# The end of layer 3 in a four-layer graph network: one buffer for two copies, transposes moved and placed in another bank, two steps exchanged, scalar operations reordered

## The chip, the cores and the metric

The kernel runs on one core of one Trainium2 chip. The metric is device microseconds of one execution; lower is better. Beside the runs there is one execution taken by the hardware profiler, and every duration below comes from it.

## What is computed

A graph of 3327 nodes with 64 features per node passes through four layers over one dense 3327 x 3327 matrix `adj`. Each layer normalises the features, applies a rectifier, computes an update and adds it to `x`. Layer 3, where the change lies, works in hyperbolic space:

```python
x_tan = _logmap0(x, C)
left = x_tan @ att_W[:D] + att_b
right = x_tan @ att_W[D:]
adj_att = jax.nn.sigmoid(left + right.T) * adj
x_local = _logmap(x[:, None, :], x[None, :, :], C)
support_t = jnp.einsum('ij,ijd->id', adj_att, x_local)
return _proj(_expmap(x, support_t, C), C)
```

`_logmap(x_i, x_j)` is a combination of the two feature vectors `x_i` and `x_j`, so the weighted sum over j falls apart into a vector part (a matrix of weights times features) and scalar sums per node. `_expmap` and `_proj` then need, per node, a few dot products, one tanh, one square root and some twenty scalar operations. The output is `x` plus a multiple of the vector sum plus a multiple of the normalised features.

## The kernel before

The nodes are padded to 26 blocks of 128. They are split in two groups: `gs_`, 12 blocks, and `gf`, 14 blocks. Layers 0 to 2 stream `adj` through SBUF. Layer 3 works in 13 phases (0 to 12) on pairs of blocks, each in two halves (`b` or `k`, 0 and 1). A phase is made of steps: `distances` (TensorE), `gelus` and `square` (ScalarE), `tanh_d` and `tanh_t` (ScalarE), `attention_*` and `factors_*` (VectorE), `gather_*` (TensorE, the vector sums) and `singles` (TensorE, the scalar sums). A step with `d` serves the pairs as they are stored; a step with `t` serves the same pairs turned, with TensorE transposes in `turned`.

The order of all these steps is written out by hand in the string `ORDER3`. `singles.12.0`, for instance, is step `singles` of phase 12, half 0. Each engine executes its own instructions in that order, and waits for others by semaphores. The last lines of `ORDER3` are the ones that matter here. After them comes `finish()`, which no other work overlaps.

The vector sums of layer 3 are kept in PSUM: `x0` (bank 2) and `x1` (bank 3) for `gf`, `x2_` (bank 1) and the upper half of `ps_` (bank 0) for `gs_`. The lower half of `ps_` holds the scalar sums of all phases but the last half. The scalar sums of that last half go into `late_`, the first 256 columns of `ends_`, a pair of banks (`pair(0)`, 1024 columns). In its second bank lies `ds_` (columns 512 to 543), the scalar sums brought to one value per node.

The steps near the end, with their lines in the profile:

- `gather_d(12, 1)` first calls `copied_singles(0, ps_)`: ScalarE copies the lower half of `ps_` into the SBUF buffer `pp_` (L1625). Its gather matmuls (shown under the helper's line, L1493) then add into the upper half of `ps_`. All `singles` matmuls are also recorded under L1493, with `p2c` as an operand.
- `singles(12, 1, 0)` takes `ends_`, clears `late_` (L1298) and adds the turned pairs' sums; `singles(12, 1, 1)` first calls `picked(0)` (L1630, matmuls of the first copied sums into `ds_`), then adds the direct pairs' sums.
- The generators `e` (`finish_s`) and `f` (`finish_f`) copy finished vector sums to SBUF (`m_t`, L1664), multiply and square them (L1595, L1666, L1667) and add the products over the features with matmuls into `drows` (L1607, in bank 2).
- `finish()` does the same for the last columns (L1678 to L1680), copies the late single sums (L1625), adds the last products (L1607), copies `drows` into the SBUF buffer `dd` (L1684), and calls `picked(1)` (L1630). `dd` and `pp_` are separate leases of one buffer, tagged `sq`. Four matmul records bring the dot products to one value per node (L1688, into `dots`, in bank 2). The vector sums are turned to node order with 13 transposes, in three calls of `by_nodes` (L1619): 4 into bank 3, 3 into the second bank of `ends_`, 6 into pair 1.
- The scalar block follows on VectorE, on operands of 128 x 26: L1706 to L1720 up to a reciprocal, the tanh on ScalarE (L1721), L1724 to L1738, the square root on ScalarE (L1739), L1740 to L1743. Its results are the scalars `ch` and `ka`.
- The output: TensorE puts `xn` into two PSUM sums (L1751), ScalarE scales the features with `ch`, block by block (L1753), TensorE adds them (L1755), VectorE multiplies the vector sums with `ka` (L1758) and adds (L1761, L1769), and SyncE stores (L1764). `sums_x` names the two PSUM sums: bank 0 for blocks 12 to 19, bank 1 for blocks 20 to 25.

The calls in `finish()` that the change moves, as they stand before:

```python
        picked(1)
        v = dots.rearrange("p (j r i h) -> p i j r h", j=2, i=2, h=2)
...
        by_nodes(gf, late_f[0], bank(3), 0, 4)
        by_nodes(gf, late_f[0], ends_[:, 5 * P :], 4, gf.n)
        by_nodes(g, m, pair(1), 0, g.n)
        sums_x = [(12, 20, bank(0)), (20, NB, bank(1)[:, : 6 * D])]
...
        V.tensor_mul(b_, ds, qs)
        V.tensor_mul(e_, ds, xq)
        V.tensor_mul(su, ss, Bq2)
```

Of the kernel before, what the change touches and what calls it, by code (L numbers as in the profile page):

```python
# [12 lines left out]
AF = mybir.ActivationFunctionType  # L13
OP = mybir.AluOpType
# [4 lines left out]
D = 64  # L19
P = 128  # L20
NB = 26
# [19 lines left out]
FAC = MIN_NORM  # L41
ATH = 8.31776613691702
MAX_NORM = 1.0 - 0.004
# [31 lines left out]
GROUPS = [Group(0, 6), Group(6, HB)]  # L75
# [149 lines left out]
def order3(text):  # L225
# [127 lines left out]
    turned.12.1.0 f tanh_d.12.0 attention_d.12.0 f singles.11.1 singles.11.0 tanh_t.12.1.0  # L353
    tanh_t.12.1.1 attention_t.12.1 e factors_t.12.1.0 turned.12.1.1 gather_t.12.1.0
    factors_d.12.0 gather_d.12.0 e factors_t.12.1.1 tanh_d.12.1 attention_d.12.1
    gather_t.12.1.1 singles.12.1.0 factors_d.12.1 singles.12.0 gather_d.12.1 gather_t.12.0.1
    singles.12.1.1 e e e e n s b f f f f f e
    """
)
# [72 lines left out]
def gnn_kernel(ctx: ExitStack, tc: tile.TileContext, t, out):  # L432
    nc = tc.nc
    V, S, G, T = nc.vector, nc.scalar, nc.gpsimd, nc.tensor
# [97 lines left out]
    ident = p0.tile([P, P], F32, name="ident")  # L532
# [75 lines left out]
    def big(g, name):  # L608

        if g.part is None:  # L610
            a = p0.tile([P, GROUPS[1].nb, D], F32, name=name, tag="b_" + name)
        else:

            if name not in bigs:
                bigs[name] = p0.tile([P, GROUPS[1].nb, D], F32, name=name, tag="b_" + name)
            a = bigs[name][:, 6 * g.part :, :]
        return a[:, : g.nb, :]

    def flat(a):
        return a.rearrange("p a d -> p (a d)")  # L620

    def pair(i):

        return ps.tile([P, 1024], F32, name="pair", tag=f"pair{i}")

    def bank(i):
        return ps.tile([P, 512], F32, name="bank", tag=f"bank{i}")
# [174 lines left out]
    gs_, gf = GROUPS  # L802
# [46 lines left out]
    for i, (ca, cb) in enumerate(starts):  # L849
        g = Group(ca, cb, part=i % 2)  # L850
# [643 lines left out]

    @step3
    def gather_d(m, b):
        nonlocal pp_
        if (m, b) == (n_all - 1, 1):
            assert ("singles", m, 0) in made3
            pp_ = flat(big(GROUPS[1], "sq"))[:, : 4 * P].rearrange("p (s i c) -> p s i c", s=2, i=2)  # L1500
            copied_singles(0, ps_)
        a = columns(dirs[m, b], PHASES[m].n)
        for c, ts, first in PHASES[m].runs:
            for p, o, lo, hi in runs(ts, place):
                for k in range(2):
                    add(
                        p[k * D : (k + 1) * D, o : o + (hi - lo) * P],
                        xd[:, 2 * c + b, :],
                        a[:, k, (first + lo) * P : (first + hi) * P],
                    )  # L1510
# [105 lines left out]
    def by_nodes(g, m, out_, lo, hi):  # L1616

        for c in range(lo, hi):
            T.transpose(  # L1619
                out_[:, (c - lo) * P : (c - lo + 1) * P], m[:, c * P : (c + 1) * P], ident  # L1620
            )
        nat.append((2 * (g.c0 + lo), 2 * (g.c0 + hi), out_[:, : (hi - lo) * P]))
# [16 lines left out]
    nat, drows, dots = [], None, None  # L1639
# [32 lines left out]
    late_ends, late_f = None, [None]  # L1672

    def finish():
        g = gs_
        m, w1, w2 = late_ends
        cs = slice(4 * P, 6 * P)
        S.activation(m[:, cs], ps_[:, 2 * P :], AF.Copy)  # L1678
        V.tensor_mul(w1[:, cs], xs[:, cs], m[:, cs])
        S.activation(w2[:, cs], m[:, cs], AF.Square)  # L1680
        copied_singles(1, late_)
        added(g, (w1, w2), 2)
        dd = flat(big(GROUPS[1], "sq"))[:, 4 * P : 6 * P]
        S.activation(dd, drows, AF.Copy)  # L1684
        picked(1)
        v = dots.rearrange("p (j r i h) -> p i j r h", j=2, i=2, h=2)
        for i in range(2):
            T.matmul(  # L1688
                v[:, i],
                lhsT=dd[:, i * P : (i + 1) * P],  # L1690
                rhs=ident.rearrange("p (j h k r) -> p j k r h", j=2, h=2, k=4)[:, :, 0],
                start=True,
                stop=True,
            )
        by_nodes(gf, late_f[0], bank(3), 0, 4)
        by_nodes(gf, late_f[0], ends_[:, 5 * P :], 4, gf.n)
        by_nodes(g, m, pair(1), 0, g.n)
        sums_x = [(12, 20, bank(0)), (20, NB, bank(1)[:, : 6 * D])]
        ds, hs, ss = ds_[:, :NB], dots[:, :NB], dots[:, 32 : 32 + NB]


        f = wide3("f", "d2")
        b_, e_, hu, su, p1, d_, Bp, th, y2, xy, ka, den, ch, n2 = (
            f[:, i * NB : (i + 1) * NB] for i in range(14)
        )
        V.tensor_mul(b_, ds, qs)  # L1706
        V.tensor_mul(e_, ds, xq)
        V.tensor_mul(su, ss, Bq2)
        V.scalar_tensor_tensor(b_, hs, 0.25 * HK, b_, op0=OP.mult, op1=OP.subtract)
        V.scalar_tensor_tensor(e_, hs, 0.25 * HK, e_, op0=OP.mult, op1=OP.subtract)  # L1710
        V.scalar_tensor_tensor(hu, hs, 0.125 * HK, B1, op0=OP.mult, op1=OP.mult)
        V.tensor_mul(d_, b_, e_)
        V.tensor_scalar(p1, su, -(FAC**2), 1.0, op0=OP.mult, op1=OP.add)
        V.tensor_sub(hu, e_, hu)

        V.scalar_tensor_tensor(Bp, d_, -(FAC**2), p1, op0=OP.mult, op1=OP.add)
        V.tensor_add(su, su, d_)
        V.scalar_tensor_tensor(th, Bp, MIN_NORM, rpn, op0=OP.max, op1=OP.mult)
        V.scalar_tensor_tensor(hu, hu, 2.0 * FAC, rpn, op0=OP.mult, op1=OP.mult)
        V.reciprocal(th, th)  # L1720
        S.activation(th, th, AF.Tanh)  # L1721


        V.tensor_mul(y2, th, th)  # L1724
        V.tensor_mul(xy, th, hu)
        V.tensor_mul(th, th, rpn)
        V.scalar_tensor_tensor(den, su, FAC**2, y2, op0=OP.mult, op1=OP.mult)
        V.scalar_tensor_tensor(n2, y2, 1.0, Bp, op0=OP.subtract, op1=OP.mult)
        V.scalar_tensor_tensor(ka, xy, 1.0, y2, op0=OP.add, op1=OP.add)
        V.scalar_tensor_tensor(den, den, 1.0, xy, op0=OP.add, op1=OP.add)  # L1730
        V.scalar_tensor_tensor(ch, ka, FAC * MAX_NORM, b_, op0=OP.mult, op1=OP.mult)
        V.scalar_tensor_tensor(n2, den, MIN_NORM, n2, op0=OP.max, op1=OP.add)
        V.tensor_scalar(den, den, MIN_NORM, None, op0=OP.max)
        V.scalar_tensor_tensor(th, Bp, MAX_NORM, th, op0=OP.mult, op1=OP.mult)
        V.tensor_mul(n2, n2, den)
        V.scalar_tensor_tensor(den, den, MAX_NORM**2, den, op0=OP.mult, op1=OP.mult)
        V.tensor_mul(ka, ka, alq)
        V.tensor_max(n2, n2, den)  # L1738
        S.activation(n2, n2, AF.Sqrt)  # L1739
        V.tensor_add(ch, ch, th)  # L1740
        V.reciprocal(n2, n2)
        V.tensor_mul(ch, ch, n2)
        V.tensor_mul(ka, ka, n2)  # L1743
        w1, w2 = (
            wide3("w", sb(n_all, b))[:, : NB * D].rearrange("p (k d) -> p k d", d=D)
            for b in range(2)
        )


        for lo, hi, a in sums_x:  # L1750
            T.matmul(a, lhsT=ident, rhs=flat(xn[:, lo:hi]), start=True, stop=False)  # L1751
        for k in [*range(12, NB), *range(6)]:
            S.activation(w2[:, k, :], h[:, k, :], AF.Copy, scale=ch[:, k : k + 1])  # L1753
        for lo, hi, a in sums_x:
            T.matmul(a, lhsT=ident, rhs=flat(w2[:, lo:hi]), start=False, stop=True)  # L1755

        def times(lo, hi, a):
            V.tensor_mul(w1[:, lo:hi], a.rearrange("p (k d) -> p k d", d=D), bc(ka[:, lo:hi]))  # L1758

        def plus(lo, hi, a):  # L1760
            V.tensor_add(w1[:, lo:hi], w1[:, lo:hi], a)  # L1761

        def store(lo, hi):
            nc.sync.dma_start(out[:, lo:hi, :], w1[:, lo:hi])  # L1764

        (_, _, a), *larger = nat[::-1]
        times(6, 12, a[:, 6 * D :])
        plus(6, 12, xn[:, 6:12])
        V.tensor_mul(w2[:, 6:12], h[:, 6:12], bc(ch[:, 6:12]))  # L1769
        plus(6, 12, w2[:, 6:12])  # L1770
        store(6, 12)
        for lo, hi, b in larger[::-1]:
            times(lo, hi, b)
        times(0, 6, a[:, : 6 * D])
        plus(0, 6, xn[:, 0:6])
        for lo, hi, b in sums_x:
            plus(lo, hi, b.rearrange("p (k d) -> p k d", d=D))
            store(lo, hi)
        plus(0, 6, w2[:, 0:6])
        store(0, 6)  # L1780
# [28 lines left out]
        nonlocal within_  # L1809
        within_ = nc.values_load(within, min_val=0, max_val=1)  # L1810

    x0 = x1 = ps_ = x2_ = late_ = ds_ = pp_ = ends_ = None
    cf = ctx.enter_context(ExitStack())
    c2 = ctx.enter_context(ExitStack())
    if True:
# [104 lines left out]
        if True:  # L1920
# [6 lines left out]
            h = n3.tile([P, NB, D], F32, name="h3")  # L1927
# [10 lines left out]
            x2, qs, pn, rpn, lefts, righth, B1, Bq2, alq, xq = (  # L1938
                n3.tile([P, NB], F32, name=n)
                for n in "x2 qs pn rpn left righth B1 Bq2 alq xq".split()  # L1940
            )
# [429 lines left out]
```

## Time and profile before

| | |
|---|---|
| median of 3 runs | 647.39 us (647.32 to 648.18) |
| the profiled execution | 643.85 us |
| its span, first to last instruction | 642.0 us |
| TensorE busy in the span | 601.1 us (94%) |
| VectorE busy | 450.2 us (70%) |
| ScalarE busy | 378.4 us (59%) |
| mean granted TensorE clock | 0.989 |
| first instruction of the scalar block (L1706) | at 625.28 us |
| first scaled block of the output (L1753) | at 630.07 us |
| end of the last VectorE instruction | at 636.55 us |

Times within the trace are microseconds from the span's start. A matrix product of 32-bit numbers shows as two records in the trace. The busy share of an engine is a mean over stages with different limits: in the last 28 us, where the change lies, the engines take turns, and what counts is what each of them waits for. The profile names those waits by the engine and line that ended them.

### The profile page before, as it was taken

Reading aid. Unit: us, or ns where it says so; the run is one execution under the profiler, and the core shown is the slowest. Engines: PE = TensorE matmul, PEld = TensorE weight load, DVE = VectorE, ACT = ScalarE, POOL = GpSimd, SP = SyncE. Lnnn points to the kernel's source line nnn. Section 1 sums busy time; section 2 is a strip of 40 time slices with the busy share of each in tenths; the row PEclk is TensorE's granted clock in tenths of the full one; section 3 lists DMA queues with packets and bytes.
Section 4 is the critical chain, followed back from the end, with each engine's and each line's share of the span. In section 5 each row is a group of like instructions: output and inputs, shape, how many; then the busy total and the mean of one; then the engine's idle time right before and its main releaser. Section 6 shows DMA issues by size and latency. Waiting matters only on the chain.

```text
span 642.0 us, 13208 instructions
## 1 busy us (share of the span) xinstructions
PE 601.1 (94%) x5592; PEld 321.8 (50%) x5592; DVE 450.2 (70%) x687; ACT 378.4 (59%) x528; POOL 25.3 (4%) x48
## 2 busy tenths in 40 slices
PE   2987999899998999999999999989999999999992
PEld 1442444334332433346777776546655555556660
DVE  3230876454488760567864866999999999999955
ACT  3110400130254420369987979999999998999734
POOL 0000000000000000030000010017000000000000
PEclk9999999999999999999999999989999999999996
DMA  8999999449998799999978895519676776755401
GB/s 334 415 417 418 364 393 339 177 157 392 418 417 368 282 415 419 417 365 400 359 277 292 300 329 225 189 58 288 206 246 211 251 235 226 240 177 196 153 2 59
DMA packets 32531, 183.40 MB, mean 286 GB/s; under 512 B 3696, under 2 KB 4752, under 8 KB 32464
## 3 DMA queue, kind: packets, MB, share of 16 engines
q1 hardware_dynamic: 32112, 181.63, 75.4%
q0 software_dynamic: 352, 0.85, 0.5%
q8 instruction: 45, 0.74, 0.5%
q14 instruction: 22, 0.18, 0.1%
HBM read 180.76 MB, written 0.85 MB: 283 GB/s over the span
## 4 chain that ended last, share of the span: by engine, by line
PE 78%; DMA 8%; DVE 6%; ACT 5%; issue 1%; SPq 0%; DVEq 0%; ACTq 0%
PE bank L772 25%; PE bank L1493 18%; PE pair L1368 8%; DMA adj<-in_adj 8%; PE bank L1886 7%; PE pair L1864 7%; PE pair L1483 4%; PE pair L873 3%; ACT w L1876 2%; PE pair L677 1%; DMA xn<-in_x 1%; PE bank L647 1%; PE bank L1755 1%; ACT tr L1438 0%; DVE mask L1833 0%
## 5 line engine op out<-in xcount | busy, mean ns | idle before, releaser
L772 PE MATMUL bank<-adj,m_a 128*64 128x384 f32 (+1 forms) x832 | 153.5, 516 | 8.9 <-DMA adj<-in_adj 6.5
L772 PEld LDWEIGHTS bank<-adj,m_a 128*64 128x64 f32 x832 | 57.1, 137 | 95.0 <-issue 71.3
L1876 ACT ACTIVATE w<-pair,ebias 128x896 uint16<-128x896 f32 (+1 forms) x100 | 90.1, 953 | 14.6 <-PE pair L1864 14.4
L772 PE MATMUL bank<-adj,m_b 128*64 128x384 f32 (+1 forms) x416 | 76.7, 515 | 1.4 <-ACT hm L861 1.4
L499 DVE SCALAR_TENSOR_TENSOR edges<-adj,edges 128x1792 bf16<-128x1792 f32 (+1 forms) x24 | 45.0, 1890 | 31.3 <-DMA adj<-in_adj 31.2
L1833 DVE TENSOR_SCALAR mask<-adj 128x1792 bf16<-128x1792 f32 (+1 forms) x52 | 51.7, 1025 | 18.4 <-PE pair L1864 18.2
L861 ACT ACTIVATE hm<-bank 64x384 f32<-64x384 f32 (+1 forms) x8 | 4.1, 512 | 94.5 <-DVE mh L860 94.2
L1886 PE MATMUL bank<-w,m_b 128*64 128x384 bf16 (+1 forms) x416 | 55.9, 340 | 0.1
L772 PEld LDWEIGHTS bank<-adj,m_b 128*64 128x64 f32 x416 | 28.8, 137 | 45.8 <-issue 41.5
L1368 PE MATMUL pair<-xs 64*128 64x384 f32 (+3 forms) x120 | 50.8, 507 | 0.5 <-ACT s L1384 0.5
L1368 PE MATMUL pair<-xs,xw 64*128 64x384 f32 (+3 forms) x120 | 50.8, 507 | 0.0
L1409 ACT ACTIVATE d<-leftb,righth 128x768 f32<-128x768 f32 (+3 forms) x45 | 38.7, 918 | 0.1
L1886 PE MATMUL bank<-w,h_t 128*64 128x384 bf16 (+1 forms) x208 | 38.2, 339 | 0.1
L1449 DVE SCALAR_TENSOR_TENSOR d<-d,adj 128x1792 f32<-128x1792 f32 x19 | 38.3, 2014 | 0.0
L1864 PE MATMUL pair<-mask,tri_b 128*64 128x384 bf16 (+1 forms) x208 | 37.0, 339 | 0.0
L1864 PE MATMUL pair<-mask,rest_a 128*64 128x384 bf16 x192 | 33.5, 341 | 0.1
L1493 PE MATMUL bank<-d,xd 128*64 128x384 f32 (+3 forms) x236 | 32.2, 411 | 0.5 <-ACT sq L1625 0.5
L1886 PEld LDWEIGHTS <-m_b 128*64 128x64 bf16 x416 | 27.3, 110 | 10.6 <-issue 1.5
L1490 DVE SCALAR_TENSOR_TENSOR tr<-pair,tr 128x1024 f32<-128x1024 f32 (+3 forms) x28 | 26.7, 954 | 4.0 <-PE pair L1483 3.5
L1438 ACT ACTIVATE tr<-leftb,righth 128x512 f32<-128x512 f32 (+1 forms) x48 | 28.7, 660 | 0.4 <-PE bank L1493 0.4
L1493 PE MATMUL bank<-d,p2c 128*32 128x128 f32 (+1 forms) x348 | 28.5, 322 | 0.0
L1864 PE MATMUL pair<-mask,tri_a 128*64 128x384 bf16 x208 | 25.8, 341 | 0.7 <-ACT w L1876 0.7
(371 smaller groups left out, 1089.0 us busy)
## 6 DMA issues: line engine op xcount, KB each, us to landing
adj<-in_adj SPq DMA_DIRECT2D x108, 896.0 KB, 6.5
adj<-in_adj SPq DMA_DIRECT2D x94, 768.0 KB, 8.7
adj<-in_adj SPq DMA_DIRECT2D x8, 640.0 KB, 5.1
adj<-in_adj SPq DMA_DIRECT2D x2, 512.0 KB, 3.9
xn<-in_x SPq DMA_DIRECT2D x3, 192.0 KB, 4.8
out<-s SPq DMA_DIRECT2D x3, 192.0 KB, 2.6
xw<-xs POOLq DMA_DIRECT2D x4, 128.0 KB, 4.9
w_l<-in_w_l SPq DMA_DIRECT2D x1, 460.0 KB, 9.9
```

What stands on the lines that cost most here:

```text
L499: V.scalar_tensor_tensor(e, a, 0.0, e, op0=OP.not_equal, op1=OP.add)
L772: T.matmul(acc[q][h * D : (h + 1) * D, : hi - lo], lhsT=m[:, k, :], rhs=a[:, h * g.w + lo : h * g.w + hi], start=first, stop=last,)
L1368: T.matmul(p[k][:, o : o + n], lhsT=l, rhs=r, start=not rows, stop=rows)
L1409: S.activation(columns(dirs[m, b], ph.n)[:, :, first * P : first * P + n], left_of(ph.g)[:, :, o : o + n], AF.Tanh, bias=righth[:, 2 * c + ...
L1438: S.activation(by_rows(a, m, u)[:, x : x + 2 * n].rearrange("p (b e) r c -> p b e r c", b=2), left_of(ph.s)[:, :, o : o + n * P].rearrange ...
L1449: V.scalar_tensor_tensor(a[:, :w], a[:, :w], 1.0, stream.tile(stream.now), op0=OP.add, op1=OP.mult)
L1490: V.scalar_tensor_tensor(a, p, rest_of(m), a, op0=OP.add, op1=OP.mult)
L1493: T.matmul(out, lhsT=lhsT, rhs=rhs, start=False, stop=True, skip_group_check=True)
L1833: V.tensor_scalar(masks[n][:, :w], a, 0.0, None, op0=OP.not_equal)
L1864: T.matmul(cnt[h][s * D : (s + 1) * D, P + lo : P + hi], lhsT=l, rhs=r, start=first and j == 0, stop=j == len(terms) - 1 or first and s == ...
L1876: S.activation(w, e, AF.Relu, bias=ebias)
L1886: T.matmul(acc2[i][q][h * D : (h + 1) * D, : hi - lo], lhsT=p[:, 2 * c + a, :], rhs=ws[n][:, h * g.w + lo : h * g.w + hi].bitcast(BF16), s ...
```

## The change

Four edits, all of them between the last steps of phase 12 and the square root of the scalar block:

1. In `ORDER3`, `singles.12.0` moves ahead of `singles.12.1.0` and `factors_d.12.1`. Before, it stood behind both.
2. The buffer for the copied single sums is taken once, in `gather_d(12, 1)`, and the copy of `drows` goes into its columns 512 to 767 under the name `dd_`. Before, `finish()` took a new lease of the same buffer for it.
3. In `finish()`, `b_` and `e_` are issued ahead of the dot product matmuls, and the 13 transposes behind the first VectorE operations that read the dot products. The three transposes of blocks 20 to 25 go to bank 0 in place of the second bank of `ends_`, and the output sum of blocks 12 to 19 goes to the first bank of pair 0 in place of bank 0.
4. The scalar operations are reordered; none is added, none is left out. `p1` goes ahead of `d_`, and `su` and `hu` behind the tanh; after the tanh, the operations that lead to the square root go first, and `ch`, `th` and `ka` go behind it. The multiplication of `th` by `rpn` moves down.

```diff
-    gather_t.12.1.1 singles.12.1.0 factors_d.12.1 singles.12.0 gather_d.12.1 gather_t.12.0.1
+    gather_t.12.1.1 singles.12.0 singles.12.1.0 factors_d.12.1 gather_d.12.1 gather_t.12.0.1
...
-            pp_ = flat(big(GROUPS[1], "sq"))[:, : 4 * P].rearrange("p (s i c) -> p s i c", s=2, i=2)
+            ends = flat(big(GROUPS[1], "sq"))
+            pp_ = ends[:, : 4 * P].rearrange("p (s i c) -> p s i c", s=2, i=2)
+            dd_ = ends[:, 4 * P : 6 * P]
             copied_singles(0, ps_)
...
-        dd = flat(big(GROUPS[1], "sq"))[:, 4 * P : 6 * P]
-        S.activation(dd, drows, AF.Copy)
+        S.activation(dd_, drows, AF.Copy)
         picked(1)
-        v = dots.rearrange("p (j r i h) -> p i j r h", j=2, i=2, h=2)
-        for i in range(2):
-            T.matmul(
-                v[:, i],
-                lhsT=dd[:, i * P : (i + 1) * P],
...
-        by_nodes(gf, late_f[0], bank(3), 0, 4)
-        by_nodes(gf, late_f[0], ends_[:, 5 * P :], 4, gf.n)
-        by_nodes(g, m, pair(1), 0, g.n)
-        sums_x = [(12, 20, bank(0)), (20, NB, bank(1)[:, : 6 * D])]
         ds, hs, ss = ds_[:, :NB], dots[:, :NB], dots[:, 32 : 32 + NB]
...
         V.tensor_mul(b_, ds, qs)
         V.tensor_mul(e_, ds, xq)
+        v = dots.rearrange("p (j r i h) -> p i j r h", j=2, i=2, h=2)
+        for i in range(2):
+            T.matmul(
+                v[:, i],
+                lhsT=dd_[:, i * P : (i + 1) * P],
...
         V.tensor_mul(su, ss, Bq2)
         V.scalar_tensor_tensor(b_, hs, 0.25 * HK, b_, op0=OP.mult, op1=OP.subtract)
         V.scalar_tensor_tensor(e_, hs, 0.25 * HK, e_, op0=OP.mult, op1=OP.subtract)
         V.scalar_tensor_tensor(hu, hs, 0.125 * HK, B1, op0=OP.mult, op1=OP.mult)
+        by_nodes(gf, late_f[0], bank(3), 0, 4)
+        by_nodes(gf, late_f[0], bank(0), 4, gf.n)
+        by_nodes(g, m, pair(1), 0, g.n)
+        sums_x = [(12, 20, pair(0)[:, :512]), (20, NB, bank(1)[:, : 6 * D])]
+        V.tensor_scalar(p1, su, -(FAC**2), 1.0, op0=OP.mult, op1=OP.add)
         V.tensor_mul(d_, b_, e_)
-        V.tensor_scalar(p1, su, -(FAC**2), 1.0, op0=OP.mult, op1=OP.add)
         V.tensor_sub(hu, e_, hu)
         V.scalar_tensor_tensor(Bp, d_, -(FAC**2), p1, op0=OP.mult, op1=OP.add)
-        V.tensor_add(su, su, d_)
         V.scalar_tensor_tensor(th, Bp, MIN_NORM, rpn, op0=OP.max, op1=OP.mult)
-        V.scalar_tensor_tensor(hu, hu, 2.0 * FAC, rpn, op0=OP.mult, op1=OP.mult)
         V.reciprocal(th, th)
         S.activation(th, th, AF.Tanh)
+        V.tensor_add(su, su, d_)
+        V.scalar_tensor_tensor(hu, hu, 2.0 * FAC, rpn, op0=OP.mult, op1=OP.mult)
         V.tensor_mul(y2, th, th)
         V.tensor_mul(xy, th, hu)
-        V.tensor_mul(th, th, rpn)
         V.scalar_tensor_tensor(den, su, FAC**2, y2, op0=OP.mult, op1=OP.mult)
         V.scalar_tensor_tensor(n2, y2, 1.0, Bp, op0=OP.subtract, op1=OP.mult)
+        V.scalar_tensor_tensor(den, den, 1.0, xy, op0=OP.add, op1=OP.add)
         V.scalar_tensor_tensor(ka, xy, 1.0, y2, op0=OP.add, op1=OP.add)
-        V.scalar_tensor_tensor(den, den, 1.0, xy, op0=OP.add, op1=OP.add)
-        V.scalar_tensor_tensor(ch, ka, FAC * MAX_NORM, b_, op0=OP.mult, op1=OP.mult)
         V.scalar_tensor_tensor(n2, den, MIN_NORM, n2, op0=OP.max, op1=OP.add)
         V.tensor_scalar(den, den, MIN_NORM, None, op0=OP.max)
-        V.scalar_tensor_tensor(th, Bp, MAX_NORM, th, op0=OP.mult, op1=OP.mult)
+        V.tensor_mul(th, th, rpn)
         V.tensor_mul(n2, n2, den)
         V.scalar_tensor_tensor(den, den, MAX_NORM**2, den, op0=OP.mult, op1=OP.mult)
-        V.tensor_mul(ka, ka, alq)
         V.tensor_max(n2, n2, den)
         S.activation(n2, n2, AF.Sqrt)
+        V.scalar_tensor_tensor(ch, ka, FAC * MAX_NORM, b_, op0=OP.mult, op1=OP.mult)
+        V.scalar_tensor_tensor(th, Bp, MAX_NORM, th, op0=OP.mult, op1=OP.mult)
+        V.tensor_mul(ka, ka, alq)
         V.tensor_add(ch, ch, th)
         V.reciprocal(n2, n2)
```

More of the change, by code (lines that the diff above doesn't have):

```diff
@@ L1496, in gather_d @@
     def gather_d(m, b):
-        nonlocal pp_
+        nonlocal pp_, dd_
         if (m, b) == (n_all - 1, 1):
             assert ("singles", m, 0) in made3
-            pp_ = flat(big(GROUPS[1], "sq"))[:, : 4 * P].rearrange("p (s i c) -> p s i c", s=2, i=2)
+            ends = flat(big(GROUPS[1], "sq"))
+            pp_ = ends[:, : 4 * P].rearrange("p (s i c) -> p s i c", s=2, i=2)
+            dd_ = ends[:, 4 * P : 6 * P]
             copied_singles(0, ps_)
@@ L1682, in finish @@
         added(g, (w1, w2), 2)
-        dd = flat(big(GROUPS[1], "sq"))[:, 4 * P : 6 * P]
-        S.activation(dd, drows, AF.Copy)
+        S.activation(dd_, drows, AF.Copy)
         picked(1)
-        v = dots.rearrange("p (j r i h) -> p i j r h", j=2, i=2, h=2)
-        for i in range(2):
-            T.matmul(
-                v[:, i],
-                lhsT=dd[:, i * P : (i + 1) * P],
[L1691 to L1694, printed above, removed]
-        by_nodes(gf, late_f[0], bank(3), 0, 4)
-        by_nodes(gf, late_f[0], ends_[:, 5 * P :], 4, gf.n)
-        by_nodes(g, m, pair(1), 0, g.n)
-        sums_x = [(12, 20, bank(0)), (20, NB, bank(1)[:, : 6 * D])]
         ds, hs, ss = ds_[:, :NB], dots[:, :NB], dots[:, 32 : 32 + NB]
@@ L1707, in finish @@
         V.tensor_mul(e_, ds, xq)
+        v = dots.rearrange("p (j r i h) -> p i j r h", j=2, i=2, h=2)
[3 more added lines that the diff above has]
+                lhsT=dd_[:, i * P : (i + 1) * P],
+                rhs=ident.rearrange("p (j h k r) -> p j k r h", j=2, h=2, k=4)[:, :, 0],
+                start=True,
+                stop=True,
+            )
         V.tensor_mul(su, ss, Bq2)
@@ L1810, in ok @@
         within_ = nc.values_load(within, min_val=0, max_val=1)
-    x0 = x1 = ps_ = x2_ = late_ = ds_ = pp_ = ends_ = None
+    x0 = x1 = ps_ = x2_ = late_ = ds_ = pp_ = dd_ = ends_ = None
     cf = ctx.enter_context(ExitStack())
```

## The prediction

> **What bounds the kernel now.** I read the page first: its span, then its chain of work, where TensorE holds 78%. Upstream of about 614 us the diff changes nothing, so only the last 28 us matter, and I asked for the chain of waits from 605 us on. Its columns are start, length, and what the chain stood on.
>
> ```profile
> 617.41 0.39 ACT sq L1625
> 617.80 0.04 issue
> 617.85 1.95 PE bank L1493 x20
> ...
> 622.63 0.56 PE pair L1630 x4
> ...
> 623.28 0.39 ACT sq L1684
> 623.67 0.04 issue
> 623.71 0.63 PE bank L1688 x4
> 624.35 0.47 PE bank L1619 x4
> 624.82 0.34 PE pair L1619 x3
> ...
> 625.28 0.10 DVE d L1706
> ```
>
> Three places show. At 617.4 TensorE stands while ScalarE copies single sums (L1625). At 622.6 to 623.7 the chain goes from `picked(1)` (L1630) to ScalarE's copy of the dot products (L1684) and back. At 624.3 to 625.2 VectorE waits for seven transposes (L1619) though none of its scalar work reads them. The answer on waits (engine, line, who ended the wait; total us, times, longest) names the same three:
>
> ```profile
> DVE d L1706 <- PE pair L1619: 4.6, 1, 4.6
> ACT sq L1684 <- PE pair L1630: 1.5, 1, 1.5
> PE bank L1493 <- ACT sq L1625: 0.5, 1, 0.5
> ```
>
> Then comes the scalar block on [128,26] operands, from VectorE's and ScalarE's timelines (start, length):
>
> ```profile
> 627.22 0.19 DVE L1724 TENSOR_TENSOR d<-d 128x26 f32<-128x26 f32 x1 [0.29 <-ACT d L1721]
> 627.33 0.18 DVE L1725 TENSOR_TENSOR d<-d 128x26 f32<-128x26 f32 x1
> 627.54 0.19 DVE L1726 TENSOR_TENSOR d<-d,rpn 128x26 f32<-128x26 f32 x1
> 627.64 0.18 DVE L1727 SCALAR_TENSOR_TENSOR d<-d 128x26 f32<-128x26 f32 x1
> ```
>
> ```profile
> 627.21 1.28 ACT L1739 ACT_TABLE_LOAD   x1
> 629.24 0.22 ACT L1739 ACTIVATE d<-d 128x26 f32<-128x26 f32 x1 [0.75 <-DVE d L1738]
> ```
>
> An independent instruction starts 0.09 to 0.11 after the one before it. One that needs the result of its direct predecessor, or overwrites what that one reads (L1726 overwrites `th`, read by L1725), starts 0.03 after its end, 0.21 in all. One that needs the result of the last but one costs some 0.12. From the block's last scalars on (L1753 at 630.07), the tail hangs on them alone.
>
> **What the Trainium skill says.** "PSUM — Partial Sum Buffer", section "PSUM bank collisions raise a hardware error": two engines may not touch one bank and quadrant at once, even at other columns, so schedulers put dependencies between them. The trace agrees: `ds` was ready at 623.20, L1706 started at 625.28, and what it waited for wrote other columns of that bank; so too the 0.48 us of the gather behind a copy of other columns of `ps_`. "VectorE: DVE Perf Modes", section "The DRAIN you can't avoid": a read after a write on the same engine needs a wait; the steps of 0.10 against 0.21 agree. "TensorE: Matmul & The Clock Gate", Part 1: the clock is halved after a quiet window of 3413 ns, and the windows run freely. The trace agrees: a half-clock stretch from 422.83 to 426.24, and the clock fell at 631.04, in the 4.83 us of idle before L1755. But the window before 422.83 was not empty (1.6 us of TensorE busy). "ScalarE: Activation LUTs", section "What ACT_TABLE_LOAD costs": 1283 ns plus a drain of some 1380. The load agrees (1.28), the drain doesn't: at 8.65 us such a load was followed by its ACTIVATE at 9.94.
>
> **The change, part by part**, on the clock of the trace before.
>
> *Singles exchanged.* `singles.12.0` (28 matmul records into `ps_`) now runs before `singles.12.1.0` (4 clearing records, 12 of singles into pair 0). No instruction is added; no DMA, and nothing on the SP or POOL queues, is moved. From 614.98 to 617.37 they take 2.4 us; 28 of the 40 singles' records are about 1.5 us, so `ps_` is ready near 616.55. The copy L1625 (0.38) ends at about 617.0, under the 0.8 us of the late singles. The gather then follows directly: the 0.48 of idle goes, and about 0.10 of pipe drain, since in an unbroken run the next group starts 0.07 to 0.17 before the one before it ends (619.41 against 619.58, 619.73 against 619.80). What is late next is VectorE's second part of `factors_d.12.1`, done at 617.44; only the gather's second half reads it. If the whole gather waited for it, it would start at 617.49. Value **0.58**, bounds 0.36 to 0.65. If the cover of late singles were gone, the 0.48 would be back.
>
> *One buffer for `pp_` and `dd_`.* The copy L1684 waited for the old buffer's last reader, L1630, ended at 623.20. Now only its data bind: L1607's last matmul ends at 622.63, so the copy runs from 622.70 to 623.08 and L1688 starts 0.05 later, at 623.13, instead of 623.71. `picked(1)` (622.56, next start possible at 623.02) lies beside it. Value **0.58**, bounds 0.53 to 0.62.
>
> *Transposes behind the dot products, in another bank; `b_` and `e_` first.* `b_` and `e_` (L1706, L1707) need only `picked(1)`: they run at about 623.3 to 623.6, beside L1688. Queued behind the waiting `b_` is the whole scalar block, which needs L1688 anyway. L1688 takes 0.63; the answer to a wait on TensorE took 0.12 (625.16 to 625.28). So `su` starts 0.75 after L1688, not 1.76 (625.47 minus 623.71). Value **1.02**, bounds 0.95 to 1.05. The 13 transposes (about 1.6 us) and the four records of L1751 (1.67) then stand beside the scalar block: L1751 ends at about 627.30 minus 1.16, 626.14, and L1755 needs it at 629.7. The new wait, L1751 for the release of pair 0 (read last by `e_`, done near 623.0), has L1751 and L1755 queued behind it; TensorE gets there at about 624.5, so it costs nothing. The cover is 3.5 us.
>
> *Scalar order.* From `su` to the tanh the chain stays `d_`, `Bp`, `th`, reciprocal: 1.13 against 1.15, counted 0. `su` and `hu` go under the reciprocal and the tanh (0.6 us free, 0.2 needed). From L1724 (0.00), with steps of 0.10, 0.12 and 0.21: `xy` 0.11, `den` 0.22, `n2` 0.32, `den` 0.43, `ka` 0.53, `n2` 0.64, `den` 0.86, `th` 0.96, `n2` 1.07, `den` 1.29, maximum 1.51, square root 1.73, against 2.02 now (629.24 minus 627.22). Then `ch`, `th`, `ka`, `ch` run beside the root, and the last starts at 1.92, so the reciprocal comes at 2.02 where the root alone would allow 1.99; now it is at 2.28. Value **0.26**, bounds 0 to 0.31: the table load ends 1.29 after the tanh, 0.45 before it is wanted, but a drain of up to 0.73 after it would be hidden now and then bind; the load at 8.65 speaks for none.
>
> *Tail.* It follows L1753 unchanged. VectorE's last wait (0.36, for L1755 at half clock) would go if the clock stayed full. TensorE's idle stretch shrinks from 4.83 to about 3.56 (626.14 to 629.70), hardly longer than one window of 3.41, but the stretch at 422.83 shows that a partly busy window can halve the clock too. Value 0, bounds 0 to 0.36.
>
> **Sum:** 0.58 + 0.58 + 1.02 + 0.26 = **2.44 us**. The profiled execution took 643.85 (span 642.0 and 1.85 around it), so it would be 641.4. The median of the runs is 647.39, 3.54 above; I take that difference as untouched: 647.39 - 2.44 = 644.95, **644.9 us**.
>
> **Rivals.** *(a) The shared buffer turns the wait around:* `picked(1)`, which follows the copy in the program, waits for it. Then it starts at 623.13 and L1688 at 623.59: 0.46 lost, 645.4. Against it: at 605.91 TensorE read one part of a `tr` tile while VectorE wrote another from 606.03 on, so SBUF is told apart by region. *(b) The move does not do what it says:* `su` still waits for the transposes. 1.02 lost, 646.0. For it: that is what L1706 does now; against: there they shared a bank, and the wait ended with the third of nine records, not the last. *(c) Two parts fail,* the exchange and the buffer for instance, 1.16 lost: 646.1. For it: short stalls often reappear at the next wait. *(d) Slower:* the exchanged singles lose the overlap of their four column groups. Now 40 records take 2.16, 0.054 each; one by one they would take some 0.17 (the gather's 16 take 1.56, 0.098 each, two at a time, so 0.195 for 256 columns, somewhat less for 128). That adds 40 x 0.116 = 4.6: 649.6. It decides once over 21 records (2.44 / 0.116) lose it. Against it: the order within each step stays, only the seam moves.
>
> **Numbers.** Forecast 0.70 (its own range 644.0 to 645.5), (a) 0.07, (b) 0.08, (c) 0.12, (d) 0.03. What can be told from no change is about 0.2%, 1.3 us, so up to 646.1: faster 0.70 + 0.07 + 0.05 of (b) + 0.06 of (c) = 0.88; same 0.09; slower 0.03. The range starts at the best bounds, 0.65 + 0.62 + 1.05 + 0.31 + 0.36 = 2.99, and 0.4 for the runs' own scatter (647.32 to 648.18), 644.0; it ends just past (b) and (c), at 646.2.
>
> **What would show it.** Right: no idle before the gather; the copy of the dot products starts within 0.1 of the last L1607 matmul; `b_` and `e_` stand apart from `su`, and `su` about 0.12 behind the dot matmuls; tanh's end to the root's start about 1.75. Wrong: a wait of `picked(1)` for ScalarE, of `su` for a transpose, of the root for its table, or a gap before L1751.

## The result, and the profile after

| | before | changed kernel |
|---|---|---|
| median of 22 runs | 646.87 us (645.04 to 649.0) | 644.76 us (641.23 to 646.95) |
| ratio of the runs | | 0.9955, 95% interval 0.9941 to 0.9970 |
| profiled execution | 643.85 us | 641.23 us |
| its span | 642.0 us | 639.4 us |

The change makes the kernel faster by 0.45% (0.30 to 0.59), which is 2.9 us (1.9 to 3.8) of the 646.87. The medians differ by 2.1 us, the profiled executions by 2.6. The forecast was 2.44 us. The runs alone can't say which part gave what: their scatter is larger than any part. The trace can, if each stage is measured from an event just ahead of it.

The chain of waits of the changed kernel, over the same stretch as before (start, length, what the chain stood on):

```profile
616.12 0.23 PE pair L1298 x4
616.35 0.77 PE pair L1493 x12
617.13 1.88 PE bank L1493 x20
...
621.84 0.55 PE pair L1632 x4
622.39 0.61 PE bank L1698 x4
623.00 0.03 issue
623.03 0.05 DVEq L1705
623.08 0.04 issue
623.12 0.18 DVE d L1705
```

ScalarE is gone from this stretch: neither the copy ahead of the gather nor that of the dot products is in the chain, and the transposes (now L1621) are gone too. From the dot products (L1698, before L1688) the chain goes straight to `su` (L1705, before L1708). The answer on waits says the same from the other side:

```profile
DVE d L1694 <- PE pair L1632: 2.6, 1, 2.6
ACT sq L1685 <- PE bank L1609: 0.9, 1, 0.9
DVE d L1705 <- PE bank L1698: 0.3, 1, 0.3
```

`b_` (L1694) waits for `picked(1)` (L1632) and no longer for transposes; the copy (L1685) waits for the product matmuls that it reads (L1609), no longer for `picked(1)`.

The stages, from the start of the last gather ahead of the singles (614.66 before, 614.10 after) to the end of the last VectorE instruction, each from the timelines' starts; the last column is what the prediction's sum took off:

| stage | before | after | saved | predicted |
|---|---|---|---|---|
| gather of the turned pairs to the gather behind the singles | 3.19 | 2.96 | 0.23 | 0.58 |
| to `picked(1)` | 4.71 | 4.71 | 0 | 0 |
| to the dot product matmuls | 1.15 | 0.59 | 0.56 | 0.58 |
| to `su` | 1.76 | 0.76 | 1.00 | 1.02 |
| to the first operation behind the tanh | 1.75 | 1.72 | 0.03 | 0 |
| to the first scaled block (L1753) | 2.85 | 2.62 | 0.23 | 0.26 |
| to the last VectorE end | 6.48 | 6.03 | 0.45 | 0, bounds 0 to 0.36 |
| sum | 21.89 | 19.39 | 2.50 | 2.44 |

Beside this, the changed kernel's profiled execution reached this stretch 0.56 us sooner and needed 0.52 us more from the last VectorE end to the end of the span (5.95 against 5.43; over all thirteen traces it lies between 5.3 and 6.3). No edit touches either.

So the sum came out almost right, and two of its terms did not: the exchange gave less than half, and the tail gave 0.45 us that was counted at nothing. That these two errors nearly cancel is luck, as the experiments show: the 0.45 us does not belong to the edits. Without it they give 2.05 us.

### The profile page after: what moved, and what is told of

Read it like the earlier page. It is cut to its first block, busy times and chain, and to the rows that moved or that the text cites. A ratio compares the mean times of both kernels' runs of the same rounds, so it can differ in the third digit from the quotient of the medians.

```text
span 639.4 us, 13208 instructions
## 1 busy us (share of the span) xinstructions
PE 599.1 (94%) x5592; PEld 321.2 (50%) x5592; DVE 450.1 (70%) x687; ACT 378.3 (59%) x528; POOL 25.2 (4%) x48
## 4 chain that ended last, share of the span: by engine, by line
PE 76%; DMA 8%; DVE 8%; ACT 5%; issue 1%; SPq 0%; DVEq 0%; ACTq 0%
PE bank L772 26%; PE bank L1493 17%; DMA adj<-in_adj 7%; PE pair L1368 7%; PE bank L1886 7%; PE pair L1864 7%; PE pair L1483 4%; PE pair L873 3%; ACT w L1876 2%; PE pair L677 1%; DMA xn<-in_x 1%; PE bank L647 1%; DVE tr L1490 0%; ACT tr L1438 0%; DVE mask L1833 0%
## 5 line engine op out<-in xcount | busy, mean ns | idle before, releaser
L772 PE MATMUL bank<-adj,m_a 128*64 128x384 f32 (+1 forms) x832 | 153.6, 516 | 8.3 <-DMA adj<-in_adj 5.9
L772 PEld LDWEIGHTS bank<-adj,m_a 128*64 128x64 f32 x832 | 57.2, 137 | 94.3 <-issue 71.8
L772 PE MATMUL bank<-adj,m_b 128*64 128x384 f32 (+1 forms) x416 | 76.7, 515 | 1.2 <-ACT hm L861 1.2
L772 PEld LDWEIGHTS bank<-adj,m_b 128*64 128x64 f32 x416 | 29.0, 137 | 45.4 <-issue 42.0
```

The source lines that it names most:

```text
L772: T.matmul(acc[q][h * D : (h + 1) * D, : hi - lo], lhsT=m[:, k, :], rhs=a[:, h * g.w + lo : h * g.w + hi], start=first, stop=last,)
```

## The experiments

Eight kernels take one part alone, undo one, or touch one suspected cost; the other three, which follow from what the first ones showed, are a short version of one, a test of its side effect, and two of the tests put together. Stages are those of the table above.

**The exchange alone**: only the line of `ORDER3`, on the kernel before.

```diff
-    gather_t.12.1.1 singles.12.1.0 factors_d.12.1 singles.12.0 gather_d.12.1 gather_t.12.0.1
+    gather_t.12.1.1 singles.12.0 singles.12.1.0 factors_d.12.1 gather_d.12.1 gather_t.12.0.1
```

> The kernel before with the two single-sum steps exchanged and nothing else. Measured from the start of the last gather of the turned pairs ahead of the singles (L1493, tr,xd, x4) to the start of the gather behind them (L1493, d,xd, x16): before 3.19 us, in the changed kernel 2.96. Prediction's sum: 2.61 (0.58 saved). Theory of the seam (TensorE changes once more between 64 and 32 columns, and loses there what it gains): 2.96, no wait for ScalarE left, and the singles with the clearing take 2.7 us and not 2.4. Rival (the gather now waits for VectorE's second part of the factors): the gather starts within 0.06 us of that part's end. All else as before: dot products to first scalar 1.76, tail as before.

Measured: 2.96 us for the first stage, and every other stage within 0.02 of before. The exchange is worth 0.23 us wherever it stands. VectorE's second part of the factors ended 2.79 after the stage's start, 0.17 before the gather, so the rival is out here.

**One buffer alone**, on the kernel before:

```diff
+            ends = flat(big(GROUPS[1], "sq"))
+            pp_ = ends[:, : 4 * P].rearrange("p (s i c) -> p s i c", s=2, i=2)
+            dd_ = ends[:, 4 * P : 6 * P]
...
-        dd = flat(big(GROUPS[1], "sq"))[:, 4 * P : 6 * P]
+        dd = dd_
```

> The kernel before with one buffer for both copies and nothing else. From the first record of the second picked (L1630) to the first dot product record (L1688): before 1.15 us. Prediction: 0.57 (0.58 saved), the copy of the dot products starting within 0.1 us of the last product matmul. Rival a (picked waits for the copy, now in the same buffer): picked starts 0.57 later than the pipe allows, and the stretch from the last product matmul to the dot products stays near 1.0.

Measured: 0.59 us instead of 1.15. The copy started 0.15 us after the start of `picked(1)` where before it was 0.72, and `picked(1)`, which stands behind the copy in the program, did not wait for it. Rival (a) of the prediction is out: in this SBUF buffer, reads and writes of different columns are told apart.

**The other bank alone**, the calls where they were:

```diff
-        by_nodes(gf, late_f[0], ends_[:, 5 * P :], 4, gf.n)
+        by_nodes(gf, late_f[0], bank(0), 4, gf.n)
...
         V.tensor_mul(e_, ds, xq)
+        sums_x = [(12, 20, pair(0)[:, :512]), (20, NB, bank(1)[:, : 6 * D])]
```

> The kernel before with the three transposes of blocks 20 to 25 in bank 0 and the output sum of blocks 12 to 19 in pair 0; the place of the calls in the program is as before. From the dot products' first record (L1688) to the scalar product su (L1708): before 1.76 us. Theory (only the shared bank made the wait): 0.75, as in the changed kernel, so this edit alone saves the whole 1.0. Rival (the calls' place in the program makes VectorE wait, rival b of the prediction): 1.5 to 1.8.

**The moved calls alone**, the banks as they were (the dot product matmuls behind `e_`, the transposes behind `hu`, as in the changed kernel):

```diff
-        by_nodes(gf, late_f[0], bank(3), 0, 4)
-        by_nodes(gf, late_f[0], ends_[:, 5 * P :], 4, gf.n)
-        by_nodes(g, m, pair(1), 0, g.n)
...
         V.scalar_tensor_tensor(hu, hs, 0.125 * HK, B1, op0=OP.mult, op1=OP.mult)
+        by_nodes(gf, late_f[0], bank(3), 0, 4)
+        by_nodes(gf, late_f[0], ends_[:, 5 * P :], 4, gf.n)
+        by_nodes(g, m, pair(1), 0, g.n)
```

> The kernel before with the transposes' calls moved behind the first readers of the dot products, b_ and e_ ahead of the dot matmuls, and the banks as before. From the dot products' first record to su: before 1.76 us. Theory: the order of the two calls on one bank decides who waits; VectorE reads first, so 0.75 here too, and the three transposes wait for nothing, since e_ has long read. Rival (both edits are needed): 1.2 or more, or a gap ahead of the transposes.

Measured: 0.77 us in both. In both, `b_` follows `picked(1)` (L1630) and `su` the dot products, and neither waits for the transposes (first the bank alone, then the moved calls alone):

```profile
625.24 0.18 DVE L1705 TENSOR_TENSOR d<-pair,qs 128x26 f32<-128x26 f32 x1 [2.63 <-PE pair L1630]
626.41 0.18 DVE L1708 TENSOR_TENSOR d<-bank,Bq 128x26 f32<-128x26 f32 x1 [0.89 <-PE bank L1688]
...
628.51 0.19 DVE L1693 TENSOR_TENSOR d<-pair,qs 128x26 f32<-128x26 f32 x1 [2.63 <-PE pair L1630]
629.68 0.18 DVE L1704 TENSOR_TENSOR d<-bank,Bq 128x26 f32<-128x26 f32 x1 [0.89 <-PE bank L1697]
```

Either edit alone saves the whole 1.0; having both adds nothing. TensorE's order is the same in all of these kernels; what differs is only whether VectorE's first read of the pair comes before or after the transposes into it in the program, or whether it is the same pair at all.

**The scalar order alone**, on the kernel before; the diff is that of the change from `p1` to the square root.

> The kernel before with the scalar operations in the new order and nothing else. From su to the first operation behind the tanh: before 1.75 us, predicted 1.73. From there to the first scaled block (L1753): before 2.85, predicted 2.59 (0.26 saved). Rival (a drain behind the table load binds, so the root can't come earlier): 2.85 stays, with the square root waiting though its operand is ready.

Measured: 1.71 and 2.61, so 0.04 and 0.24 saved. The square root started 1.75 after the first operation behind the tanh, against 2.02; the table load costs nothing here, and no drain shows. In the changed kernel:

```profile
624.59 0.22 ACT L1719 ACTIVATE d<-d 128x26 f32<-128x26 f32 x1 [2.28 <-DVE d L1718]
624.83 1.28 ACT L1736 ACT_TABLE_LOAD   x1
626.60 0.22 ACT L1736 ACTIVATE d<-d 128x26 f32<-128x26 f32 x1 [0.49 <-DVE d L1735]
```

The load ends at 626.11, and the root waits 0.49 more for its operand: there is still slack.

**The changed kernel without the exchange**: only the line of `ORDER3` as before.

> The changed kernel with the two single-sum steps in the order of before. From the gather ahead of the singles to the gather behind them: seam theory 3.19 us, against 2.96 in the changed kernel, so 0.2 us longer in all. The other stages as in the changed kernel (0.59 from picked to the dot products, 0.76 to su, 2.62 from the tanh to the scaled blocks). In the runs the difference of 0.04% to the changed kernel can't be told: 0.995 to 0.997 of before. Prediction's sum: 0.58 longer.

Measured: 3.18 us for the first stage, the others as in the changed kernel, except the tail (6.49). In the runs 0.9968 of before (0.9950 to 0.9986), which does not part it from the changed kernel.

**Why the exchange gives 0.23.** TensorE's timelines have the answer (start, length, operands; `bank` is a tile of one PSUM bank and `pair` one of two; `128*32` and `128*64` are rows and columns that the matmul uses). Before:

```profile
614.98 0.30 PE L1298 MATMUL pair<-identb,rest_a 64*64 64x128 bf16 x4
615.21 0.73 PE L1493 MATMUL pair<-tr,p2c 128*32 128x256 f32 x10
615.68 0.39 PE L1493 MATMUL bank<-dir,p2c 128*32 128x256 f32 x2
615.78 0.28 PE L1493 MATMUL pair<-tr,p2c 128*32 128x128 f32 x2
...
616.98 0.39 PE L1493 MATMUL bank<-dir,p2c 128*32 128x128 f32 x4
617.85 1.73 PE L1493 MATMUL bank<-d,xd 128*64 128x256 f32 x16 [0.48 <-ACT sq L1625]
```

The changed kernel:

```profile
614.10 0.39 PE L1493 MATMUL bank<-tr,xd 128*64 128x128 f32 x4
614.42 0.41 PE L1493 MATMUL bank<-dir,p2c 128*32 128x256 f32 x2
...
615.52 0.60 PE L1493 MATMUL bank<-dir,p2c 128*32 128x256 f32 x6
616.05 0.30 PE L1298 MATMUL pair<-identb,rest_a 64*64 64x128 bf16 x4
616.28 0.84 PE L1493 MATMUL pair<-tr,p2c 128*32 128x256 f32 x12
617.06 1.74 PE L1493 MATMUL bank<-d,xd 128*64 128x256 f32 x16
```

Singles of 32 columns run four at a time. Before, the clearing (L1298, 64 columns) came first and the two halves' singles followed without a break: the first `bank` singles started at 615.68 while `pair` singles ran to 616.06. Now the clearing lies between them. The first half's singles run out (they end at 616.12, and the clearing starts only 0.07 before that), the clearing takes its 0.23, and the late singles, only 12 records, start up four column groups anew and run out again ahead of the gather. The singles with the clearing take from 614.42 to 617.12, 2.70 us, where they took from 614.98 to 617.37, 2.39. Of the 0.48 us of idle and 0.06 of overlap won, 0.31 is given back. The test moves the clearing away from between them, ahead of the gather of phase 12's first half:

```diff
+    @step3
+    def ends():
+        nonlocal late_, ds_, ends_
+        ends_ = pair(0)
+        late_ = ends_[:, : 2 * P]
+        cleared(late_)
+        ds_ = ends_[:, 512:544]
...
-    factors_d.12.0 gather_d.12.0 e factors_t.12.1.1
+    factors_d.12.0 ends gather_d.12.0 e factors_t.12.1.1
```

> The changed kernel with the clearing of the late sums moved up, ahead of the gather for which TensorE waits 0.4 us anyway, so that the singles of both halves stand side by side at one column width. From the gather ahead of the singles to the gather behind them: seam theory about 2.5 us against 2.96 (the clearing's 0.23 and one change of width, some 0.2). Rival (the gather waits for VectorE's second part of the factors or for ScalarE's copies): 2.8 or more. In the runs 0.9945 to 0.9960 of before, at most 0.07% better than the changed kernel.

Measured: 2.51 us. TensorE and its weight loads (`PEld`) in this kernel:

```profile
619.31 0.39 PE L1493 MATMUL bank<-dir,p2c 128*32 128x256 f32 x2
619.33 0.39 PE L1493 MATMUL pair<-tr,p2c 128*32 128x256 f32 x2
619.53 0.28 PE L1493 MATMUL bank<-dir,p2c 128*32 128x128 f32 x2
619.54 0.39 PE L1493 MATMUL pair<-tr,p2c 128*32 128x256 f32 x2
619.64 0.28 PE L1493 MATMUL bank<-dir,p2c 128*32 128x128 f32 x2
619.75 0.60 PE L1493 MATMUL pair<-tr,p2c 128*32 128x256 f32 x8
620.40 1.74 PE L1493 MATMUL bank<-d,xd 128*64 128x256 f32 x16
```

```profile
620.40 0.63 PEld L1493 LDWEIGHTS bank<-d,xd 128*64 128x64 f32 x8 [0.52 <-ACT sq L1629]
```

`bank` and `pair` singles overlap again, and with the clearing gone from between them the singles take 2.14 us (618.21 to 620.35), 0.33 less than the 2.47 that they took with it, its own 0.23 left out. Of that 0.33, 0.11 is lost again: the gather now follows ScalarE's copy (L1629, ended at 620.34) and starts 0.05 behind the last single, not 0.06 ahead of its end. It started at 620.40, while VectorE's second part of the factors ended only at 620.43, so it does not wait for that. The copy's cover is used up, and little more is to be had from this order.

The stage of 2.51 us leaves out what the clearing costs in its new place. TensorE there, in the changed kernel and then in this one:

```profile
611.53 1.08 PE L1493 MATMUL bank<-tr,xd 128*64 128x256 f32 x8
612.53 1.73 PE L1493 MATMUL bank<-dir,xd 128*64 128x256 f32 x16
...
615.08 1.08 PE L1493 MATMUL bank<-tr,xd 128*64 128x256 f32 x8
616.10 0.30 PE L1298 MATMUL pair<-identb,rest_a 64*64 64x128 bf16 x4
616.33 1.74 PE L1493 MATMUL bank<-dir,xd 128*64 128x256 f32 x16
```

From the first gather to the second it is 1.00 us without the clearing and 1.25 with it. The 0.4 us of waiting named in the expectation was one of the weight loads; the matmuls of the gather ahead were still running then. So the clearing costs its time there too, and the early clearing saves about 0.2 us in all, not 0.45 (from the transposes L1483 ahead of both gathers to the gather behind the singles: 5.80 in the changed kernel, 5.58 in this one). In the runs it is 0.9960 of before (0.9939 to 0.9981).

**The clock in the tail.** More matmuls, whose results nobody reads, in TensorE's idle stretch of the kernel before:

```diff
+        for _ in range(16):
+            T.matmul(ends_[:, : 2 * P], lhsT=ident, rhs=flat(xn[:, 0:4]), start=True, stop=True)
         for k in [*range(12, NB), *range(6)]:
             S.activation(w2[:, k, :], h[:, k, :], AF.Copy, scale=ch[:, k : k + 1])
```

> The kernel before with 16 more matmuls (32 records, 128x256) between the first addends of the output sums and the rest, into an unused part of PSUM; nothing reads them. They keep TensorE at work in the 4.83 us in which it was idle. Clock theory (VectorE's last wait of 0.36 us came from the half clock of the last four matmuls): the clock stays full, the wait is gone, and from the first scaled block to the last VectorE end it takes 6.1 us and not 6.48. Rival (the wait comes from ScalarE's scaled blocks): 6.4 to 6.5 at full clock too.

Measured: 7.32 us. I had sized it wrongly: the 32 records took 7.07 us, so the output sums started behind them, only at 634.90, and VectorE waited for them:

```profile
DVE s L1760 <- PE pair L1753: 1.2, 1, 1.2
```

Without that wait it would be 6.11, but such a subtraction proves little. The short version has 8 matmuls, into bank 2:

```diff
+        spare = bank(2)[:, : 2 * P]
+        for _ in range(8):
+            T.matmul(spare, lhsT=ident, rhs=flat(xn[:, 0:4]), start=True, stop=True)
```

> As e6_warm, but 8 matmuls (16 records, some 3.5 us at the 0.22 us each that e6_warm showed) and into bank 2, which nobody reads any more. Clock theory: TensorE's clock stays full through the output sums, their last four records end within 1.7 us of work, VectorE's wait of 0.36 us is gone, and from the first scaled block to the last VectorE end it takes 6.0 to 6.25 us, not 6.48. Rival (the wait comes from ScalarE's scaled blocks or from the stores): 6.4 to 6.5.

Measured: 6.03 us, and the wait is gone with ScalarE's blocks as they were, so the rival is out. TensorE at the end of this kernel:

```profile
629.27 3.62 PE L1754 MATMUL bank<-xn,ident 128*128 128x256 f32 x16
634.27 1.12 PE L1758 MATMUL bank<-s,ident 128*128 128x512 f32 x2 [1.38 <-ACT s L1756]
635.70 0.91 PE L1758 MATMUL bank<-s,ident 128*128 128x384 f32 x2 [0.30 <-ACT s L1756]
```

The last pair took 0.91 us at full clock. In the kernel before, all four records at half clock took 3.35, and VectorE waited; in the changed kernel the last pair took 1.42:

```profile
632.14 3.35 PE L1755 MATMUL bank<-s,ident 128*128 128x512 f32 x4 [4.83 <-ACT s L1753]
635.53 0.55 DVE L1761 TENSOR_TENSOR s<-s,bank 128x384 f32<-128x384 f32 x1 [0.36 <-PE bank L1755]
...
629.53 1.13 PE L1755 MATMUL pair<-s,ident 128*128 128x512 f32 x2 [3.59 <-ACT s L1753]
630.97 1.42 PE L1755 MATMUL bank<-s,ident 128*128 128x384 f32 x2 [0.31 <-ACT s L1753]
```

In the changed kernel the granted clock fell (from 1.00 to 0.50) at 631.23, in the middle of that pair, just late enough for VectorE not to wait. Eleven of the traces fall in three classes. Where the clock fell before the first of these matmuls, the tail took 6.48 to 6.50 us (the kernel before, the exchange alone, the buffer alone, the changed kernel without the exchange, the early clearing, the test with the first bank). Where it fell 0.3 to 0.8 us after their start, 6.21 to 6.24 (the bank alone, the moved calls alone, the scalar order alone). Where it fell 1.7 us after or not at all, 6.03 (the changed kernel and the short test above). So the 0.45 of the tail is no part of the change in itself: it depends on when the clock falls. Whether the shorter idle stretch (3.59 against 4.83) makes the good case likelier is not shown. Of the three traces that have it and no added matmuls, the clock fell late in one (the changed kernel) and early in two (without the exchange; early clearing).

**Bank or tile?** The wait in the long version above was odd: VectorE read the second bank of the pair, and the matmuls wrote the first. The test, on the kernel before:

```diff
-        by_nodes(gf, late_f[0], ends_[:, 5 * P :], 4, gf.n)
+        by_nodes(gf, late_f[0], ends_[:, : 3 * P], 4, gf.n)
```

> The kernel before with the three transposes of blocks 20 to 25 in the first bank of the pair and not in the second, in which ds lies; nothing else is changed. From the dot products' first record to su: before 1.76 us. If the wait was one for the bank: 0.75 to 0.8. If it is one for the whole tile of two banks, as the 1.21 us in e6_warm suggest (there VectorE, reading the second bank, waited for matmuls into the first): 1.76.

Measured: 1.76 us. VectorE waited for the transposes as before, though they now wrote another bank than the one it read:

```profile
628.91 0.18 DVE L1706 TENSOR_TENSOR d<-pair,qs 128x26 f32<-128x26 f32 x1 [4.59 <-PE pair L1619]
```

So the wait reaches across the whole tile of two banks. In the SBUF buffer of the second experiment, two column ranges did not wait for each other.

**Early clearing and a warm clock together**, on the changed kernel: the step `ends` and six such matmuls.

> e8_early with 6 such matmuls (2.6 us of TensorE's idle 3.4) behind the first addends. Clock theory: full clock in every run, whatever the phase of the clock's window, so the tail takes 6.0 to 6.25 us, and from the gather ahead of the singles to the last VectorE end it takes 18.95 to 19.15 us, against 19.39 in the changed kernel's profile. Rival (the added matmuls delay the output sums): over 19.4. In the runs 0.994 to 0.996 of before, too near the changed kernel to be told from it.

Measured: 18.95 us from the gather to the last VectorE end (2.51 for the first stage, 6.03 for the tail), just at the lower end of what was expected, against 19.39 in the changed kernel's trace and 21.89 before. What the clearing costs stands ahead of this stretch here too. Measured from the transposes ahead of it (L1483), it is 22.02 us against 22.23 in the changed kernel and 24.73 before. In the runs it is 0.9951 of before (0.9936 to 0.9966), median 643.61 us of 22. It is the shortest of these over that stretch; the runs do not part it from the changed kernel.

## Where the prediction was wrong, and where it was right

Three of its terms failed. The exchange was put at 0.58 us and gave 0.23. The tail was put at 0 and gave 0.45 in the changed kernel's trace. And the starting figure, 647.39 us with 0.4 us for scatter, came from three runs; 22 runs gave 646.87, and a far wider scatter. That the trace's 2.50 us lies so near to 2.44 is luck, since the first two errors nearly cancel and the tail's 0.45 is not the edits' own. The other three terms came within 0.03 us, through the waits that were named.

- **One buffer: right.** 0.56 in the changed kernel and alone, for 0.58. The copy followed the last product matmul by 0.08 us, as written.
- **Transposes and bank: right in size, in part wrong in the cause.** 1.00 for 1.02. I costed the two edits as one and did not see that either is enough. I also read the wait as one for a shared bank, from the Trainium skill's "PSUM bank collisions raise a hardware error" in "PSUM — Partial Sum Buffer". The wait exists in the same form between the two banks of one tile (1.76 us), so it follows the tile as the program declares it. By that page the bank is why such waits are put in; it does not say how far this one reaches. Rival (b) is out: `su` waited for the dot products alone, and no gap stood ahead of L1751.
- **Scalar order: right.** 0.26 in sum (0.03 and 0.23) for 0.26; root at 1.76 for 1.73. The bound of 0, for a drain behind the table load, did not come about.
- **Exchange: the mechanism held, its size failed.** The step said "The gather then follows directly: the 0.48 of idle goes, and about 0.10 of pipe drain". The idle went. But I took "they take 2.4 us" over from the old order for the new one, with the clearing still at the front; it moved in between, and they took 2.70. Rival (d), a lost overlap of the column groups, was given 4.6 us or nothing; at the seam alone it was real and cost 0.31. The measured 0.23 lies below the lower bound of 0.36, which had looked only at VectorE. Of rival (c), two parts that fail, only this one came in part.
- **Tail: counted at 0, came to 0.45.** The step named the reason (the clock) and the bound, 0.36; the short test shows the same 0.45 (6.48 to 6.03) from a full clock alone, so the cause was right and the bound too low. VectorE's wait of 0.36 is counted from the end of the instruction ahead of it; without a wait the next one starts 0.09 before that end (632.47 against 631.88 and 0.68 in the changed kernel), and that 0.09 is won too. Counting 0 as the likeliest was a choice on the clock's phase, which the spread of 6.03 to 6.50 over the traces leaves open.
- **The starting figure and the range: failed.** The step said "The median of the runs is 647.39, 3.54 above; I take that difference as untouched". Twenty-two runs of the kernel before have a median of 646.87, 0.52 lower, which is more than the whole 0.4 us that the range allowed for scatter. That 0.4 came from three runs that lay 0.86 apart; twenty-two of the changed kernel lie 5.7 apart. The plain median, 644.76, is inside the range, but the ratio applied to 646.87 gives 643.96, just below its lower end of 644.0. As far as the traces show, the scatter arises upstream, in code that all thirteen kernels share: the last records of layers 0 and 1 (L772) start anywhere from 280.0 (changed kernel) to 285.8 us (moved calls alone). TensorE's idle time there behind the loads of `adj`, for one of the two groups, is 5.9 us in the first and 9.1 in the second. Then a half-clock stretch near 423 us comes in six traces, which costs about 0.2 us where it lasts 3.41 and 1.7 where it lasts 6.83. Of the 0.56 us by which the changed kernel's profile was ahead at 614 us, 0.38 was there at L772.

What stays open is the 2.9 us that the ratio gives against the 2.5 of the trace, or the 2.05 without the tail. The interval (1.9 to 3.8) holds all three, so the runs neither call for a further cause nor say how often the tail's 0.45 comes.

## What to carry to other kernels

When a step is moved away from its neighbours, cost it with what now stands before and behind it: a duration read from an unbroken run of like matmuls is not the duration of the same matmuls with another tile shape in between. A wait on a tile can be lifted by changing the tile or by changing the order of the two calls in the program, even where the engines' own order stays as it is. And where single runs of a kernel scatter by more than the change is worth, measure each stage in the trace from an event just ahead of it and of every place to which an edit moves work, and take the range's term for scatter from more than three runs.

## What was not expected of the hardware

- Matmuls of another tile shape, put into a run of like ones, cost more than their own time. Moving the four clearing matmuls (0.23 us) out from between two groups of singles made the singles 0.33 us shorter beside that, of which 0.22 was left in the sum. Whether it is the columns (64 and 32), the rows or the type (bf16 and f32) was not tested.
- A half-clock stretch needs no empty stretch ahead of it. In the kernel before, TensorE had been at work for 1.6 of the 3.41 us ahead of the fall at 422.83, and in the 12 us before it never stood idle for longer than 1.32. The other five traces with such a stretch near 423 us show the same.
- In this chain of operations on 26 columns one rule holds closely: steps of 0.09 to 0.11 us, 0.12 for one that needs the result of the last but one, 0.21 for one that needs that of the last. Worked out so on paper, the 12 instructions up to the square root came to 1.73 us; measured were 1.76.
